# Deformable attention and bottleneck over eight images: x of the next image on GpSimd's queue, q's preparation in four steps, sample transposes half a round later

## The chip, the cores and the metric

The kernel runs on one core of a Trainium2 chip. A core has a matrix engine (TensorE, called PE in the profile, with its weight loads listed as PEld), a vector engine (DVE), an activation engine (ACT), GpSimd (POOL) and SyncE (SP), which here only starts transfers. Each engine works through its own list of instructions in the order in which the program put them there, and an instruction at the head of a list that waits holds up everything behind it. Transfers between HBM and SBUF are started by SP or by POOL and are moved by 16 DMA engines that all of them share.

The metric is the device time of one execution in microseconds (us), the median over several runs. Lower is better.

## The reference, cut to what matters

Two layers work on x, of shape (8, 512, 64, 64): eight images, 512 channels, 4096 pixels. Layer 0 is an attention with sampled keys. Layer 1 is a small bottleneck of convolutions and two dense products.

```python
# layer 0
x0 = groupnorm(x)                                  # 32 groups
q  = w_q @ x0                                      # 512 x 512, per pixel
off = tanh(w_off2 @ gelu(w_off1 * q[:, ::4, ::4])) * 4.0    # 16 x 16 sample places per head
kv = w_kv @ grid_sample_bilinear(q, places(off))   # 256 keys and values
x  = x + w_out @ softmax((q * scale) @ k.T) @ v + b_out     # 8 heads of 64
# layer 1
y = depthwise_conv(conv1x1(groupnorm(x)))          # 512 -> 32 channels, 64x64 -> 32x32
y = fc2(fc1(y))                                    # over the 1024 places
x = x + conv1x1(depthwise_deconv(y))               # 32 -> 512 channels
```

Everything is in float32. The group norm of an image needs the statistics of the whole image before its first q can be computed.

## The kernel before, in words

**Tiling.** An image is held in SBUF as [128 partitions, 4 channel blocks, 4096 pixels] and cut into 8 tiles (`t`) of 512 pixels. There are two such regions and one spare tile for each; image b lives in region b % 2. A tile of x, of q and of the output sits one place further down or up in the same region (`x_tile`, `q_tile`, `out_tile`), so that the stages overwrite each other's input.

**The main loop.** For each image there are 32 rounds (`r`), one per pixel tile and pair of heads (`hp`). A round g emits, in this order: the scaling of earlier results (`scale_two`, every second round before, every other after), the product of weights and values (PE `pa`, L474), the sum of exponentials (PE `pn`, L501, every second round), the logits of the next round (PE `ps`, L456) with their exponentials on ACT (`es`, L464), then, six rounds late (`LAG`), the output projection (PE `pp`, L543) whose result DVE adds to the residual (L550, L553). The residual x is read again from HBM by SP (`load_residual`, L532), and each finished tile is stored by SP (`store`, L556). For tile t of the output these come at r % 4 = 1 (store, first half of the next residual) and r % 4 = 2 (second half).

**Work beside the rounds.** A generator `next_image(b)` gives out other work in small steps. It is called twice in a round: before the output projection (`phase[0] = 0`) and after it (`phase[0] = 1`). I call each call a slot; slot 0 is r = 5, second half, slot 1 is r = 6, first half, and so on. For b = 1 to 6 three things run there:

- `first`: layer 1 of image b-1. Slots 0 to 10 hold its statistics, the product `py` (slot 3, L626), the load of fc1's weights by SP (slot 3, L660, 1 MB), the convolution and the dense products (`pz`, `ph` L690, `pht`, `pu`). In the second halves from slot 12 to slot 26 `project_beside` makes eight output pieces, k = 0 to 7: PE `po` (L766), ACT adds the bias (L791 into one shared half tile called `both`, shown as `spare`, and L796 into two `part` tiles), and POOL starts three transfers of together 1 MB that add the pieces to the output in HBM (L801). `both` is a single buffer, so the L791 of piece k+1 waits until the `both` transfer of piece k has landed. The last piece, k = 7, uses `part` tiles only.
- the loads of x of image n = b+1 (`load_x`, L191), eight of 1 MB, into the region which image b-1 leaves. Before, SP starts them, at slots 5, 8, 9, 10, 11, 12, 16 and 17. Two slots after the last one SP loads w_q (`load_wq`, L135, 1 MB).
- the statistics of x of image n (`norm_x`, L196, 32 operations of DVE, six per second half from slot 12 on, so that they are used up at slot 22), and then three steps of `project_q`: (1) DVE aggregates (`mv`, L167); (2) PE sums over groups (`gps`, L171) and DVE takes differences (`dv`); (3) PE sums again (`gpsb`, L180), DVE adds eps (`ve`, L182), POOL takes the power -0.5 (`gs`, L183), and DVE normalises the first tile of x (L208, four operations). Tiles 1 to 7 are normalised by POOL later.

When `first` is at its end (slot 26), slot 27 emits the whole projection of q as one block (PE `pq`, L251, and the transposes `pqt`, L226), some 125 us on PE, between rounds 19 and 20. In the rounds after it `sample` runs: POOL gathers q by rows (L395), DVE weighs them (`weigh`, L361 to L366), and `to_channels` transposes the result on PE (`pf`, L371), once for each half of the keys. `project_k` (L409) reads them at r = 30.

**What sets the order.** It is written by hand: the program is traced in the order of the calls and each engine gets its own list in that order. A DMA that SP or POOL starts is one entry in that engine's list and waits there for the data, for the buffer, and for the transfer that used the same one of eight counters before, that is the one eight transfers back on the same queue.

Of the kernel before, what the change touches and what calls it, by code (L numbers as in the profile page):

```python
# [19 lines left out]
NCC = C // P  # L20
HW = 64
N = HW * HW
TP = 512
NT = N // TP
# [25 lines left out]
def kernel(  # L50
# [15 lines left out]
    nc = tc.nc  # L66
    xs = x.rearrange("b (cc p) n -> b p cc n", p=P)
# [25 lines left out]
    place = {b: b for b in range(B)}  # L93
    region = {b: b % 2 for b in range(B)}

    def spot(b, k):
        j = region[b]
        k %= NT + 1
        return spares[j] if k == 0 else regions[j][:, :, (k - 1) * TP : k * TP]

    def x_tile(b, t):
        return spot(b, t + 1)
# [59 lines left out]
    def group_stats(st, which, b):  # L162

        nm = f"{which}_{b}"
        mv = small.tile([P, NCC, 2], F32, tag="mv", name=f"mv{nm}")
        for cc in range(NCC):
            nc.vector.bn_aggr(mv[:, cc, :], st[:, cc].rearrange("p t s -> p (t s)"))  # L167
        mean, var = mv[:, :, 0], mv[:, :, 1]
        yield None
        gps = ps_mm.tile([P, TP], F32, tag="mm", name=f"gps{nm}")  # L170
        nc.tensor.matmul(gps[:, :NCC], cst[:, K_GRP : K_GRP + P], mean, start=True, stop=True)  # L171
        gs = small.tile([P, 2, NCC], F32, tag=f"gs{which}", name=f"gs{nm}")
        nc.vector.tensor_copy(gs[:, 0], gps[:, :NCC])
        dv = small.tile([P, NCC], F32, tag="dv", name=f"dv{nm}")
        nc.vector.tensor_sub(dv, mean, gs[:, 0])
        nc.vector.tensor_mul(dv, dv, dv)
        nc.vector.tensor_add(dv, dv, var)
        yield None
        gps2 = ps_mm.tile([P, TP], F32, tag="mm", name=f"gpsb{nm}")
        nc.tensor.matmul(gps2[:, :NCC], cst[:, K_GRP : K_GRP + P], dv, start=True, stop=True)  # L180
        ve = small.tile([P, NCC], F32, tag="ve", name=f"ve{nm}")
        nc.vector.tensor_scalar_add(ve, gps2[:, :NCC], EPS)  # L182
        nc.gpsimd.tensor_tensor(gs[:, 1], ve, nhalf, ALU.pow)  # L183
        return gs
# [1 line left out]

    both_pools = ((t2, "t2"), (gp, "g"))

    def load_x(b, order=range(NT)):
        for t in order:  # L190
            nc.sync.dma_start(x_tile(b, t), xs[place[b]][:, :, t * TP : (t + 1) * TP])  # L191

    def norm_x(b, st, order=range(NT)):
        for t in order:
# [4 lines left out]
    def project_q(b, st, mq, qd, pools):  # L199

        gs = yield from group_stats(st, 0, b)

        qd_px = qd.rearrange("(g h p j) d -> h p g (j d)", g=HEADS, p=P, j=2)

        def normalise(t):
            xt = x_tile(b, t)
            for cc in range(NCC):
                (nc.gpsimd if t else nc.vector).tensor_scalar(  # L208
                    xt[:, cc, :],
                    xt[:, cc, :],  # L210
                    gs[:, 0, cc : cc + 1],
                    gs[:, 1, cc : cc + 1],
                    ALU.subtract,
                    ALU.mult,
                )

        def by_pixel(t, k, bank=(ps_a, "pa")):

            h, ch = divmod(k, 2)
            px = q_tile(b, t)[:, :, 2 * P * h : 2 * P * (h + 1)].rearrange(  # L220
                "p c (n j) -> p c j n", j=2
            )
            pt = bank[0].tile([P, 2, 2 * P], F32, tag=bank[1], name=f"pqt_{b}_{t}_{k}")
            for j in range(2):
                for i in range(2):
                    nc.tensor.transpose(  # L226
                        pt[:, j, i * P : (i + 1) * P], px[:, 2 * ch + i, j, :], ident
                    )
            pool, tag = pools[k % len(pools)]
            qr = pool.tile([P, C], F32, tag=tag, name=f"qr_{b}_{t}_{k}")  # L230
            qr_out = qr.rearrange("p (g j d) -> p j g d", j=2, d=DH)
            qr_in = pt.rearrange("p j (g d) -> p j g d", d=DH)
            if k % 2:
                nc.vector.tensor_copy(qr_out, qr_in)  # L234
            else:
                nc.scalar.copy(qr_out, qr_in)
            nc.sync.dma_start(
                qd_px[2 * t + h, :, 4 * ch : 4 * ch + 4, :],
                qr.rearrange("p (g m) -> p g m", g=4),
            )  # L240

        normalise(0)
        yield None
        for t in range(NT):
            xt, qt = x_tile(b, t), q_tile(b, t)
            if t + 1 < NT:
                normalise(t + 1)
            for oc in range(NCC):
                pq = ps_mm.tile([P, TP], F32, tag="mm", name=f"pq_{b}_{t}_{oc}")
                for cc in range(NCC):  # L250
                    nc.tensor.matmul(  # L251
                        pq,
                        wbuf[:, cc, oc * P : (oc + 1) * P],
                        xt[:, cc, :],
                        start=(cc == 0),
                        stop=(cc == NCC - 1),
                    )
                nc.scalar.copy(qt[:, oc, :], pq)  # L258
                yield 4
                if t:  # L260
                    by_pixel(t - 1, oc)
                    yield 0.64
            if mq is not None:
                nc.vector.tensor_reduce(
                    mq[:, t, :], qt, axis=AX.X, op=ALU.max, apply_absolute_value=True
                )
        for q in range(NQ):
            by_pixel(NT - 1, q, ((ps_a, "pa"), (ps_mm, "mm"))[q % 2])
            yield 0.64
# [8 lines left out]
    def sample(b, qd):  # L278
# [101 lines left out]

        steps = [(h, half, ky) for h in range(2) for half in range(2) for ky in range(2)]

        for slot in range(2 * len(steps) + 3):
            n, odd = divmod(slot, 2)
            if not odd and n >= 5 and n % 4 == 1:
                to_channels(n // 4 - 1)
            if odd and n >= 1:
                weigh(*steps[n - 1], held.pop(0))
            if n < len(steps):
                h, half, ky = steps[n]  # L390
                if not odd:
                    held.append(gp.tile([P, 4, 2, DH], F32, tag="g", name=f"g_{b}_{n}"))
                for i in (2 * odd, 2 * odd + 1):
                    k = h * HEADS + 4 * half + i
                    nc.gpsimd.indirect_dma_start(  # L395
                        held[-1][:, i, :, :].rearrange("p j d -> p (j d)"),
                        None,
                        qd[:, :],
                        bass.IndirectOffsetOnAxis(ap=row[:, ky, k : k + 1], axis=0),
                    )  # L400
            yield None
# [451 lines left out]
    def next_image(b):  # L853

        n = b + 1
        if b:
            free = spot(b - 1, 0)
            first = layer1(b - 1, st1s.pop(b - 1), project_beside, free, free[:, 0:2, :])
            other = iter(())
            if n < B:  # L860
                st = new_stats(0, n)
                blocks = norm_x(n, st)
                other = ready_q(n, st)

            loads = {slot: t for t, slot in enumerate((5, 8, 9, 10, 11, 12, 16, 17))}
            first_block = 12
            ahead = 3
            slot = 0  # L870
            while first:
                if next(first, "end") == "end":
                    first = None
                if n < B:
                    if slot in loads:
                        load_x(n, (loads[slot],))
                    if slot == max(loads) + 2:
                        load_wq()
                    if slot >= first_block and phase[0]:
                        for _ in range(6):  # L880
                            if blocks and next(blocks, "end") == "end":
                                blocks = None
                    if blocks is None and ahead:
                        next(other)
                        ahead -= 1
                slot += 1
                yield None
            yield from other
        if n < B:
            yield from sample(n, qds[n])  # L890
# [10 lines left out]
    with tc.manual_schedule():  # L901
# [13 lines left out]
        for n, step in enumerate(ready_q(0, st)):  # L915
            if n == 3 * NCC:
                st = new_stats(0, 1)
                blocks, other = norm_x(1, st), ready_q(1, st)
            if n >= 3 * NCC and next(blocks, "end") == "end" and 13 * NCC <= n < 13 * NCC + 3:
                next(other)  # L920
        room = 0
        for step in sample(0, qds[0]):
# [7 lines left out]
        for g in range(len(names) + LAG):  # L930
            b, r = divmod(g, ROUNDS)
# [67 lines left out]
    with tc.If(large > 0):  # L999
        with tc.For_i(0, B, 1) as i:  # L1000
            b = "m"
# [94 lines left out]
```

## Time and profile before

| | us |
|---|---|
| median of 3 runs | 3451.34 |
| range of the runs | 3450.25 to 3452.16 |
| the profiled execution, device time | 3462.55 |
| its span, first to last instruction | 3460.8 |
| one image in steady state (`py` at 1891.1 to `py` at 2313.3) | 422.2 |
| idle time of PE before its first `gps`, at the start | 30.0 |

How to read the profile: "busy" is time in which an engine worked. A line of the timeline gives the start in us, the time that the merged instructions took, engine, line and operation, out<-in, the count, and in brackets how long the engine had been idle before it and what ended that wait. A line of the windows view gives a stretch, its length, the busy time of PE, PEld, DVE, ACT and POOL in it, the TensorE clock that was granted (1.00 is full speed), the mean busy share of the 16 DMA engines, and GB/s moved. The list of waits gives who waited for whom, the total, the number of times and the longest.

The page's rows on DMA queues and issues are shown below: packets, MB, and the time their packets took as a share of 16 engines' span (q1 is SP's hardware queue, q0 POOL's software queue); then the loads of x, of which 48 of the 64 belong to the six images in question, and the transfers that add to the output.

```profile
q1 hardware_dynamic: 265712, 312.05, 27.6%
q0 software_dynamic: 39664, 75.53, 12.3%
...
image<-in_x_dram SPq DMA_DIRECT2D x64, 1024.0 KB
...
out_dram<-part POOLq DMA_DIRECT2D x126, 256.0 KB
out_dram<-spare POOLq DMA_DIRECT2D x49, 512.0 KB
```

### The profile page before, as it was taken

How to read it: one execution, taken by the hardware profiler on the slowest of the kernel's cores; microseconds unless marked ns; L12 is line 12 of the kernel's file. 1: busy time of each engine (PE TensorE's matmuls, PEld its weight loads, DVE VectorE, ACT ScalarE, POOL GpSimd, SP SyncE). 2: the span in 40 equal slices, each digit the busy share in tenths (PEclk: the TensorE clock that was granted, in tenths of full speed). 3: DMA queues.
4: the chain of work that ended last, by engine and by line, in shares of the span. 5: the costliest groups of instructions: out<-in, count | busy, mean ns of one | idle time of the engine just before them, and what ended most of it. 6: DMA issues, size and time to landing. Idle time of an engine off the chain costs nothing.

```text
span 3460.8 us, 42052 instructions
## 1 busy us (share of the span) xinstructions
PE 3333.0 (96%) x16660; PEld 1240.7 (36%) x16660; DVE 1895.2 (55%) x2958; ACT 1093.3 (32%) x1512; POOL 931.3 (27%) x685
## 2 busy tenths in 40 slices
PE   6999999999999999999999999999999999999996
PEld 3554223335332352324433244332443324433222
DVE  4433665742757327574275833658246682466565
ACT  1224333332433323333232423324233342332420
POOL 6180400152401614017030170302712027120201
PEclk9999999999999999999999999999999999999996
DMA  7222221662327523275232842329332292322613
GB/s 274 73 79 68 74 74 62 188 154 69 102 82 204 127 76 99 85 216 104 82 98 86 220 96 76 110 74 235 88 96 82 89 250 64 96 76 86 123 38 135
DMA packets 305582, 390.35 MB, mean 113 GB/s; under 512 B 17760, under 2 KB 157280, under 8 KB 305376
## 3 DMA queue, kind: packets, MB, share of 16 engines
q1 hardware_dynamic: 265712, 312.05, 27.6%
q0 software_dynamic: 39664, 75.53, 12.3%
q8 instruction: 132, 2.16, 0.3%
q14 instruction: 74, 0.61, 0.1%
HBM read 193.52 MB, written 192.94 MB: 112 GB/s over the span
## 4 chain that ended last, share of the span: by engine, by line
PE 80%; issue 10%; POOL 3%; DVE 3%; DMA 2%; ACT 1%; SPq 0%; POOLq 0%; DVEq 0%; ACTq 0%
PE pq L251 25%; PE pp L543 20%; PE ps L456 11%; PE pa L474 11%; PE pqt L226 3%; POOL out_dram L801 3%; PE pn L501 3%; PE py L626 2%; PE pk L409 2%; PE pv L436 2%; DMA image<-in_x_dram 1%; PE po L766 1%; DVE rb L527 1%; DVE image L529 0%; PE po L303 0%
## 5 line engine op out<-in xcount | busy, mean ns | idle before, releaser
L251 PE MATMUL pq<-image,wbuf 128*128 128x512 f32 x2048 | 919.9, 594 | 2.4 <-DVE image L208 1.9
L543 PE MATMUL pp<-image,wout 128*64 128x512 f32 x3584 | 827.4, 602 | 19.8 <-DVE image L529 19.0
L464 ACT ACTIVATE es<-ps 128x1024 f32<-128x1024 f32 x512 | 503.5, 1022 | 294.6 <-PE ps L456 212.6
L251 PEld LDWEIGHTS pq<-image,wbuf 128*128 128x128 f32 x2048 | 374.5, 192 | 391.3 <-issue 384.1
L474 PE MATMUL pa<-es,vt 128*64 128x512 f32 x2048 | 490.1, 599 | 4.8 <-ACT es L464 4.8
L395 POOL DMA_INDIRECT g<-qd,row x256 | 272.2, 1063 | 776.7 <-PE pp L543 531.5
L208 POOL TENSOR_SCALAR image<-image,gs 128x512 f32<-128x512 f32 x224 | 465.0, 2653 | 0.4
L456 PE MATMUL ps<-image,kt 64*64 64x512 f32 x3584 | 443.6, 609 | 22.1 <-ACT spare L791 21.7
L543 PEld LDWEIGHTS pp<-image,wout 128*64 128x64 f32 x3584 | 237.2, 137 | 579.7 <-issue 481.0
L234 DVE COPY qr<-pqt 128x512 f32<-128x512 f32 x128 | 88.4, 691 | 634.5 <-PE pqt L226 622.9
L550 DVE SCALAR_TENSOR_TENSOR image<-pp,vec,image 128x512 f32<-128x512 f32 x224 | 167.2, 746 | 441.9 <-PE pp L543 420.4
L486 DVE TENSOR_TENSOR es<-es,es 128x1024 f32<-128x1024 f32 x256 | 310.5, 1213 | 78.8 <-PE pa L474 77.3
L258 ACT COPY image<-pq 128x512 f32<-128x512 f32 x224 | 131.1, 585 | 685.0 <-PE pq L251 665.5
L481 ACT COPY image<-pa 128x512 f32<-128x512 f32 x224 | 131.4, 587 | 617.7 <-PE pa L474 562.7
L183 POOL TENSOR_TENSOR gs<-ve,nhalf 128x4 f32<-128x4 f32 x16 | 22.6, 1414 | 1015.1 <-DVE ve L182 1015.1
L474 PEld LDWEIGHTS pa<-es,vt 128*64 128x64 f32 x2048 | 136.0, 136 | 290.9 <-issue 263.3
L456 PEld LDWEIGHTS ps<-image,kt 64*64 64x64 f32 x3584 | 114.8, 132 | 334.9 <-issue 180.2
L801 POOL DMA_DIRECT2D out_dram<-spare x49 | 59.6, 1217 | 629.8 <-ACT spare L791 623.2
L514 DVE RECIPROCAL rn<-pn 128x512 f32<-128x512 f32 x64 | 214.7, 3354 | 11.8 <-PE pn L501 9.1
L527 DVE STREAM_SHUFFLE rb<-rn 128x512 f32<-128x512 f32 x256 | 186.6, 729 | 0.1
L226 PEld LDWEIGHTS pqt<-ident,image 128*128 128x128 f32 x896 | 137.9, 203 | 100.1 <-issue 89.0
L196 DVE BATCH_NORM_STATS2 st<-image 128x6 f32<-128x512 f32 x256 | 156.8, 677 | 7.7 <-DMA image<-in_x_dram 7.6
(148 smaller groups left out, 2454.7 us busy)
## 6 DMA issues: line engine op xcount, KB each, us to landing
image<-in_x_dram SPq DMA_DIRECT2D x64, 1024.0 KB
qd<-qr SPq DMA_DIRECT2D x256, 256.0 KB
image<-in_x_dram SPq DMA_DIRECT2D x112, 512.0 KB
out_dram<-image SPq DMA_DIRECT2D x49, 1024.0 KB
out_dram<-part POOLq DMA_DIRECT2D x126, 256.0 KB
out_dram<-spare POOLq DMA_DIRECT2D x49, 512.0 KB
wbuf<-in_w_kvT_dram SPq DMA_DIRECT2D x14, 1024.0 KB
spare<-in_x_dram SPq DMA_DIRECT2D x16, 512.0 KB
```

The lines of the kernel that those rows point to most:

```text
L208: (nc.gpsimd if t else nc.vector).tensor_scalar(xt[:, cc, :], xt[:, cc, :], gs[:, 0, cc : cc + 1], gs[:, 1, cc : cc + 1], ALU.subtract, AL ...
L226: nc.tensor.transpose(pt[:, j, i * P : (i + 1) * P], px[:, 2 * ch + i, j, :], ident)
L251: nc.tensor.matmul(pq, wbuf[:, cc, oc * P : (oc + 1) * P], xt[:, cc, :], start=(cc == 0), stop=(cc == NCC - 1),)
L395: nc.gpsimd.indirect_dma_start(held[-1][:, i, :, :].rearrange("p j d -> p (j d)"), None, qd[:, :], bass.IndirectOffsetOnAxis(ap=row[:, ky, ...
L456: nc.tensor.matmul(ps[k : k + DH, a, :], kt[r : r + DH, hp, kc * P + k : kc * P + k + DH], qt[r : r + DH, hp, :], start=True, stop=True,)
L464: nc.scalar.activation(e, ps, AF.Exp)
L474: nc.tensor.matmul(pa[a * DH : (a + 1) * DH, :], vt[:, kc, hd * DH : (hd + 1) * DH], es[kc][:, a, :], start=(kc == 0), stop=(kc == 1),)
L486: nc.vector.tensor_add(es[0], es[0], es[1])
L514: nc.vector.reciprocal(rn, denominators.pop((b, t)))
L527: nc.vector.stream_shuffle(rb, rn, [2 * (hp % 2) + hp // 2] * 32)
L543: nc.tensor.matmul(pp[r : r + DH, :], wout[:, hp, oc * P + r : oc * P + r + DH], ao[:, hp, :], start=(hp == 0), stop=(hp == NCC - 1),)
L550: nc.vector.scalar_tensor_tensor(xt[:, oc, :], pp, col(V_BOUT + oc), xt[:, oc, :], ALU.add, ALU.add)
```

## The change

The diff has three parts.

1. `load_x` takes a queue. In `next_image` the eight loads of x are started by POOL, one in each of the slots 5 to 12, where SP had started them at 5, 8 to 12, 16 and 17. `load_wq` stays at slot 19 (5 + 8 + 6) and on SP.
2. `project_q` gets one more `yield` ahead of the first normalisation, so that its preparation has four steps: the normalisation of the first tile is a step of its own. The steps stand at the head of a slot, ahead of `first`, where they had stood at its end. The statistics still end in slot 22, so the steps come in slots 23, 24, 25 and 26 where they had come at the end of 22, 23 and 24. The prologue takes four steps instead of three as well.
3. In `sample` the transposes `to_channels` move from the even slot 2n to the odd slot 2n+1 (n = 5 and 9), and there is one more slot in the loop. The condition of `weigh` is written anew so that nothing is weighed in the additional slot.

```diff
-    def load_x(b, order=range(NT)):
+    def load_x(b, order=range(NT), queue=nc.sync):
         for t in order:
-            nc.sync.dma_start(x_tile(b, t), xs[place[b]][:, :, t * TP : (t + 1) * TP])
+            queue.dma_start(x_tile(b, t), xs[place[b]][:, :, t * TP : (t + 1) * TP])
@@ project_q
+        yield None
         normalise(0)
         yield None
@@ sample
-        for slot in range(2 * len(steps) + 3):
+        for slot in range(2 * len(steps) + 4):
             n, odd = divmod(slot, 2)
-            if not odd and n >= 5 and n % 4 == 1:
+            if odd and n >= 5 and n % 4 == 1:
                 to_channels(n // 4 - 1)
-            if odd and n >= 1:
+            if odd and 1 <= n <= len(steps):
                 weigh(*steps[n - 1], held.pop(0))
@@ next_image
-            other = iter(())
+            other, blocks = iter(()), ()
...
-            loads = {slot: t for t, slot in enumerate((5, 8, 9, 10, 11, 12, 16, 17))}
+            first_load = 5
             first_block = 12
-            ahead = 3
+            ahead = 4
             slot = 0
             while first:
+                if blocks is None and ahead:
+                    next(other)
+                    ahead -= 1
                 if next(first, "end") == "end":
                     first = None
                 if n < B:
-                    if slot in loads:
-                        load_x(n, (loads[slot],))
-                    if slot == max(loads) + 2:
+                    if first_load <= slot < first_load + NT:
+                        load_x(n, (slot - first_load,), nc.gpsimd)
+                    if slot == first_load + NT + 6:
                         load_wq()
                     if slot >= first_block and phase[0]:
                         for _ in range(6):
                             if blocks and next(blocks, "end") == "end":
                                 blocks = None
-                    if blocks is None and ahead:
-                        next(other)
-                        ahead -= 1
                 slot += 1
                 yield None
@@ prologue
-            if n >= 3 * NCC and next(blocks, "end") == "end" and 13 * NCC <= n < 13 * NCC + 3:
+            if n >= 3 * NCC and next(blocks, "end") == "end" and 13 * NCC <= n < 13 * NCC + 4:
                 next(other)
```

In the lists of the engines this gives, for each of six images: POOL's list has seven loads of x between its `gs` of layer 1 and the three transfers of piece k = 0, and the eighth after these three; SP's list has no load of x; DVE's aggregation, differences and first normalisation stand later, the first normalisation behind the L550 and L553 of round 18 and no longer ahead of two `scale_two` pairs; PE's `gps` stands just ahead of the `po` of piece 6, and `gpsb` ahead of the output projection of round 18; `pf` stands after the logits of the next round and ahead of its output projection.

## Prediction

> **What bounds the kernel now.** I read the busy table first, then the list of waits, then the timelines of PE, ACT, DVE, POOL and SP through one image, and last the windows, for what the DMA engines do meanwhile. PE is busy 3333.0 of 3460.8 us. Of its 127.8 us without work 30.0 lie at the start; the rest is what an edit of order can win, with the half clock that follows a gap. The list of waits:
>
> ```profile
> PE 3333.0 (96%) x16660; PEld 1240.7 (36%) x16660; DVE 1895.2 (55%) x2958; ACT 1093.3 (32%) x1512; POOL 931.3 (27%) x685
> ...
> ACT spare L791 <- DMA out_dram<-spare: 74.6, 11, 8.2
> ...
> DVE image L208 <- POOL gs L183: 33.1, 8, 5.4
> ...
> PE ps L456 <- ACT spare L791: 21.7, 8, 3.8
> ...
> PE pp L543 <- DVE image L529: 19.0, 15, 2.3
> ```
>
> PE waits for `both` (21.7 us) and for DVE L529 (19.0), and DVE stood before L529 for `gs` of POOL (33.1). In the third image:
>
> ```profile
> 1965.08 1.94 PE L474 MATMUL pa<-es,vt 128*64 128x512 f32 x8
> ...
> 1969.52 2.74 PE L456 MATMUL ps<-image,kt 64*64 64x512 f32 x16 [2.50 <-ACT spare L791]
> 1972.19 4.80 PE L543 MATMUL pp<-image,wout 128*64 128x512 f32 x16
> 1976.93 1.14 PE L766 MATMUL po<-spare,outw 32*128 32x512 f32 x8
> ...
> 2001.16 1.94 PE L543 MATMUL pp<-image,wout 128*64 128x512 f32 x8
> 2005.10 3.56 PE L543 MATMUL pp<-image,wout 128*64 128x512 f32 x8 [2.00 <-DVE image L529]
> 2008.58 1.16 PE L766 MATMUL po<-spare,outw 32*128 32x512 f32 x8
> ```
>
> A stall costs its gap and a slow stretch after it (`pp` 4.80 for some 3.65, `ps` 2.74 for 1.95). So I measure each by how much longer its round is than one without a stall, over the six images:
> - Stall 1 (piece k = 3): `pa` to `po` 1965.08 to 1976.93 is 11.85 us, where an unstalled round has 7.33. Excess 4.67, 3.09, 5.48, 4.51, 3.12, 5.32: 26.2 us.
> - Stall 2 (k = 4), in the second and fifth image only: 3.69 + 3.83 = 7.5 us.
> - Stall 3 (first normalisation): `pp` 2001.16 to 2008.58 is 7.42, against 3.58. Excess 3.20, 2.86, 2.86, 3.84, 2.85, 2.88: 18.5 us.
> - Stall 4: `pf` waits for `weigh`, 7.8 us, with no slow clock after it.
>
> ```profile
> L371 PE MATMUL pf<-ident,image 128*128 128x128 f32 x64 | 11.7, 290 | 7.8 <-DVE image L366 7.8
> ```
>
> Behind stall 3 is DVE's wait for POOL's L183 (2.21 us, from 1999.51); behind stall 1 a transfer:
>
> ```profile
> 2001.76 1.92 DVE L208 TENSOR_SCALAR image<-image,gs 128x512 f32<-128x512 f32 x4 [5.06 <-POOL gs L183]
> ```
> ```profile
> 1968.36 1.11 ACT L791 ACTIVATE spare<-po,vec 128x1024 f32<-128x1024 f32 x1 [6.96 <-DMA out_dram<-spare]
> ```
>
> SP had put 5 MB beside that 1 MB of k = 2 (a store 1, residual halves 0.5 each, x 2, w_q 1):
>
> ```profile
> 1955.82 0.38 SPq L556 DMA_DIRECT2D out_dram<-spare  x1
> 1956.30 0.45 SPq L532 DMA_DIRECT2D image<-in_x_dram  x1
> 1956.80 2.38 SPq L191 DMA_DIRECT2D image<-in_x_dram  x2
> 1959.28 0.76 SPq L532 DMA_DIRECT2D image<-in_x_dram  x1
> 1960.14 0.72 SPq L135 DMA_DIRECT2D wbuf<-in_w_qT_dram  x1
> ```
>
> The windows (PE, PEld, DVE, ACT, POOL, clock, DMA share, GB/s) show loads of x alone, then pieces alone, then both:
>
> ```profile
> 1930.00:1935.00 5.00, 5.00 (x32) 1.43 (x30) 4.79 (x12) 1.61 (x2) 0.00 (x0) 1.00 1.05 388
> 1950.00:1955.00 5.00, 5.00 (x32) 1.37 (x24) 4.89 (x9) 2.05 (x2) 1.56 (x2) 1.00 1.04 154
> 1965.00:1970.00 5.00, 2.50 (x16) 0.69 (x16) 5.00 (x8) 1.65 (x3) 0.24 (x1) 1.00 1.10 265
> ```
>
> **What the Trainium skill says.** "DMA: Bandwidth & Descriptors", Queues, rings and completion order: each DMA engine goes round the queue rows that have work, packet by packet. The trace agrees: mixed, 265 GB/s lie between 388 and 154. The same page, Issuing engines are not separate DMA queues: another issuing engine gives no other DMA engines. "SBUF — State Buffer", SBUF: two separate sides: some DVE operations keep GpSimd from writing descriptors, and a transfer that it starts then appears blocked. The trace of before cannot confirm it for loads, as POOL starts none there. "TensorE: Matmul & The Clock Gate", What's actually happening: half clock after an idle window of about 3.4 us. Here it follows gaps of 2.0 and 2.5 us already; the measurement decides.
>
> **The change part by part.**
>
> *Preparation of q.* No operation is added; `gps` comes a step later, L208 three slots later. After it, POOL's 2.21 us begin with `gpsb` ahead of `pp` of round 18, which takes 3.65 us, and L208 stands behind the L550 and L553 of that round, which wait for this `pp` anyway. So the 5.06 us of DVE's wait lie under `pp`. L208 takes 1.92 us and, with an L550 (0.75) ahead of it, ends some 3.5 us after `pp`; PE comes to the projection of q 4.8 us after `pp`, behind an L474 and L456. That is 1.3 us to spare; if it fails, the price is its excess, under 2 us an image. Stall 3 goes: 18.5 us. What is late next is the second exponential on ACT, 5.06 us after, for which DVE's L486 is ready at 4.7.
>
> *`pf` half a round later.* Behind `ps` (1.95 us) the result of `weigh` has been there (the longest wait was 1.75 for a pair). The copies behind `pf` end some 2.6 us after it, `pk` reads them at 4.3. Stall 4 goes: 7.8 us.
>
> *The loads.* SP's list loses 48 issues, POOL's gains them. POOL has room: it waited 49.23 us before piece k = 0.
>
> ```profile
> 1939.03 1.38 POOL L801 DMA_DIRECT2D out_dram<-spare  x1 [49.23 <-ACT spare L791]
> ```
>
> An L801 of half a load's size takes 1.2 to 1.4 us, so seven loads are 7 x 1.2 = 8.4 us if the issue doesn't grow with size, 7 x 2.4 = 17 if it does: hidden. Behind a load that waits stand only loads and k = 0. Nothing holds POOL to the slots of the code, since slots order lists and not times: x0 to x6 need only PE past `py` and the old stores landed, which I read as 1894.5 to 1898, not 1900 to 1927. 7 MB at 2.7 us each (388 GB/s) are 19 us: they end about 1917. Their bound on the other side is the skill's price for a transfer that GpSimd starts ("DMA: Bandwidth & Descriptors", Bandwidth): 6.15 us for 1 MB, thus 43 us, to 1938, an estimate. I take 19 us, as the 16 engines are the same. x7 stands behind k = 0 and runs from about 1942 to 1948, when k = 1 starts (1948.6).
>
> In the stretch 1895 to 1917 the engines had room before (in 1898 to 1906 the windows give a DMA share of 0.41), but fc1's weights run there, for this product:
>
> ```profile
> 1914.66 1.07 PE L690 MATMUL ph<-spare,wbuf 128*32 128x256 f32 x16
> ```
>
> The weights are issued at 1898.15 and a load of them lands in 6.91 us elsewhere in the chain of waits. With half of the engines they need some 10 to 14 us at most and are there by 1912, before 1914.66. The small transfers for `rn` (1912.9 to 1914.8) come at the end of the burst; DVE has about 2.2 us free after them. Cost between 0 and 8.2 us an image (below); I take 0.
>
> *Does stall 1 go?* Ahead of k = 2's landing SP keeps 3 MB without x (store, residuals, w_q). Up to that landing at 1968.36, of 12.5 us at 260 GB/s (3.2 MB), 1 MB with its slower adds took about a third of the packets, and SP's queue had moved only some 2.7 MB. So as long as SP has 2.7 MB or more queued, the piece has the same share and lands at the same time. Another piece, k = 6, issued at 1997.67 beside 2 MB of SP (a store and two residual halves), landed at about 2009.3, 11.6 us later, as k = 2's 11.4.
>
> w_q stays at slot 19, where it meets k = 2 as before. Bounds for stall 1: nothing wins 0, all 26.2; I take 0. Stall 2 needs a backlog of more than 3 MB and goes: 7.5 us (bounds 0 and 7.5).
>
> *Sum.* 18.5 + 7.8 + 7.5 = 33.8 us. The profiled device time is 3462.55 (span 3460.8, and 1.75 around it), 11.2 above the median; 3462.55 - 33.8 = 3428.8, and against the median 3451.3 - 33.8 = 3417.5 us.
>
> **Rivals.**
> - *Stall 1 goes too.* For it: SP's queue is 2 MB shorter when k = 2 lands. Against: k = 6 above. All four stalls: 60.0 us, 3391.3.
> - *The early burst costs a part.* x7 delays k = 1 (an L791 has 1.6 us to spare there), or `rn` comes late to DVE. Of 33.8, 10 to 25 us stay: 3426 to 3441.
> - *Slower: fc1's weights are starved.* One mechanism: the burst of 7 MB holds the engines, and 1 MB on SP's queue lands only when it is through, about 1921. PE's list stands at `ph` for 1921 - 1914.7 = 6.3 us, with 1.9 for the half clock 8.2 us, six times 49: 3451.3 - 33.8 + 49 = 3467. It decides from 33.8 / 6 = 5.6 us an image. For it: nothing spreads the loads out, and the price of 43 us would last beyond `ph`. Against: engines go round the queues.
> - *The change does nothing for PE:* the gaps move to the next wait, 3451. Against: three of the four have slack of 1 us or more behind them.
>
> **How the numbers follow.** A measurement here tells 0.2%, 6.9 us, from no change. Forecast 0.58, its own range 3407 to 3425 (stall 1 shortened by up to 10 us below; above, stall 2 left); stall 1 gone 0.12; burst costs a part 0.15; weights starved 0.11; nothing 0.04. The range takes in the two faster rivals and leaves out 0.15 with the last two: 3390 to 3441. Faster 0.58 + 0.12 + 0.15 = 0.85, same 0.04, slower 0.11.
>
> **What would show it.** After: DVE L208 no longer waits for `gs`, and PE `pp` not for L529; the row of `pf` has no idle time; POOL issues x0 to x6 at about 1895 in the third image and `ph` does not wait for its weights; ACT L791 still waits 6 to 7 us at k = 3, and PE `ps` for it about 15 us in all. I am wrong if `ph` or DVE L527 waits more, if x7 pushes k = 1 back, or if the wait of `ps` for L791 is gone.

## The result, and the profile after

The changed kernel is slower: 3463.2 us (median of 8 runs, 3459.65 to 3464.47) against 3451.0 (8 runs of before), a ratio of 1.0034 with a 95% interval of 1.0023 to 1.0045. That is 12 us more, where 34 less were forecast. Of the later experiments' executions two slow ones, of 4939.5 and 5605.6 us at granted clocks of 0.65 and 0.57, are not counted. Line numbers of the changed kernel are one higher from L251 on: L791 is now L792, L796 is L797, L527 is L528.

The page's busy table and the list of waits (who waited for whom, total, number, longest) of the changed kernel:

```profile
PE 3344.5 (97%) x16660; PEld 1246.7 (36%) x16660; DVE 1897.0 (55%) x2958; ACT 1092.1 (32%) x1512; POOL 966.7 (28%) x733
```
```profile
ACT es L465 <- DVE es L487: 82.9, 33, 5.4
...
ACT spare L792 <- DMA out_dram<-spare: 43.4, 6, 8.1
...
DVE rb L528 <- DMA rn<-rn: 31.9, 9, 4.4
...
PE ps L457 <- ACT spare L792: 16.6, 6, 3.6
...
PE po L767 <- ACT es L465: 12.5, 6, 2.1
ACT part L797 <- DMA out_dram<-part: 10.8, 12, 2.1
PE ps L457 <- ACT part L797: 10.1, 6, 2.5
```

Three waits that were to go are gone from the six images: L208 no longer waits for `gs`, `pp` no longer for L530, and `pf` no longer for `weigh`. In their place PE waits in each of the six images twice anew: `po` for an exponential (12.5 us) and `ps` for the `part` copies (10.1). The same list of the kernel before has DVE's wait for `rn` at 11.9 us, and neither `po` for L464 nor `ps` for L796 among PE's waits:

```profile
ACT es L464 <- DVE es L486: 65.0, 35, 2.9
...
DVE rb L527 <- DMA rn<-rn: 11.9, 9, 2.7
```

To see where the time went, I cut each of the six image periods at PE's `po` of each piece and summed each stage over the six images of one profiled execution, in us. "k0" is the stretch from `po` of k = 0 to `po` of k = 1. The last stage is cut once more, at the end of the projection's `pq` and `pqt`.

| stage | before | after | difference |
|---|---|---|---|
| `py` to k0 | 272.2 | 272.2 | 0 |
| k0 | 57.2 | 82.1 | +24.9 |
| k1, k2, k5 | 160.6 | 160.6 | 0 |
| k3 (stall 1) | 76.6 | 78.8 | +2.2 |
| k4 (stall 2) | 63.9 | 56.4 | -7.5 |
| k6 (stall 3) | 76.7 | 58.3 | -18.4 |
| k7 to the projection of q | 28.9 | 41.0 | +12.1 |
| the projection of q | 760.6 | 764.9 | +4.3 |
| its end to the next `py` (`pf`) | 1042.7 | 1031.6 | -11.1 |
| six periods | 2539.4 | 2545.9 | +6.5 |

So all that was to be removed was removed: 18.4, 7.5 and 11.1 us, where 18.5, 7.5 and 7.8 were forecast. Two new losses outweigh it: 24.9 us at k0, and 12.1 + 4.3 = 16.4 us at k7 and in the projection behind it.

**The first loss: `rn` behind the burst.** POOL starts x0 to x6 at once, as forecast (timeline of POOL, third image, changed kernel):

```profile
1890.57 0.84 POOL L191 DMA_DIRECT2D image<-in_x_dram  x1 [5.20 <-PE py L627]
1894.03 4.54 POOL L191 DMA_DIRECT2D image<-in_x_dram  x6 [2.62 <-PE py L627]
1936.42 1.27 POOL L802 DMA_DIRECT2D out_dram<-spare  x1 [37.86 <-ACT spare L792]
```

The windows (length, busy time of PE, PEld, DVE, ACT, POOL, clock, DMA share, GB/s) show the 16 engines full until about 1914:

```profile
1902.00:1906.00 4.00, 4.00 (x24) 1.06 (x16) 3.89 (x6) 1.74 (x2) 0.00 (x0) 1.00 1.02 384
1906.00:1910.00 4.00, 4.00 (x28) 1.20 (x26) 3.96 (x5) 1.03 (x2) 0.00 (x0) 1.00 1.03 388
1910.00:1914.00 4.00, 4.00 (x34) 1.48 (x32) 1.20 (x2) 1.86 (x3) 0.00 (x0) 1.00 1.04 390
1914.00:1918.00 4.00, 4.00 (x26) 1.16 (x20) 2.41 (x6) 0.58 (x1) 0.00 (x0) 1.00 0.19 71
```

SP issues the four small transfers for `rn` (4 KB each) at 1908.47, inside the burst. From there to DVE's L528, which reads them, it took 3.7 us before (1912.91 to 1916.60) and takes 7.0 us now. The records of single packets show where: in all six images the first packet of a transfer comes about 4.1 us after its issue, where it came 1.2 us after it before. The difference of 2.9 us is close to the 2.7 us in which one load of 1 MB passes at 388 GB/s. That a transfer waits for about one load is my reading of these two numbers; no run tests it with loads of another size. DVE's list is then 3 us late for 17 us on end, and passes that to ACT and PE (timelines of DVE, ACT and PE, changed kernel):

```profile
1915.47 0.01 DVE L528 LOAD_MASK_SELECT rb<-rn  x1 [4.27 <-DMA rn<-rn]
...
1932.78 1.22 DVE L487 TENSOR_TENSOR es<-es,es 128x1024 f32<-128x1024 f32 x1
```
```profile
1934.10 1.02 ACT L465 ACTIVATE es<-ps 128x1024 f32<-128x1024 f32 x1 [5.38 <-DVE es L487]
1935.02 1.11 ACT L792 ACTIVATE spare<-po,vec 128x1024 f32<-128x1024 f32 x1
```
```profile
1931.99 1.13 PE L767 MATMUL po<-spare,outw 32*128 32x512 f32 x4
1935.17 1.85 PE L767 MATMUL po<-spare,outw 32*128 32x512 f32 x4 [2.05 <-ACT es L465]
1936.95 3.68 PE L475 MATMUL pa<-es,vt 128*64 128x512 f32 x8
```

Read from the bottom: the second half of `po` needs the bank of PSUM that the second exponential reads; that exponential overwrites the tile which L487 adds; L487 stands in DVE's list behind everything that waited for `rn`. From `py`, L487 came at 43.1 us before and at 46.2 now. So PE is late by the same 3.0 us: the second half of `po` begins 3.18 us after the first in the third image, where it began 0.15 us after it before. (The gap shows as 2.05 us only, because the halves otherwise overlap.) In three images that is all. In the three others the clock falls to half behind the gap, for 3.4, 3.4 and 6.8 us, and the loss is 4.7, 4.7 and 6.3 us; in the third image, shown here, `pa` takes 3.68 us for 1.94.

**The second loss: k = 7 behind k = 6.** With stall 3 gone PE comes to k = 7 earlier, and ACT's L797 meets the `part` tiles of k = 6, which POOL had started to send from 2000.24 on (timeline of ACT, then of PE, changed kernel):

```profile
2007.83 1.26 ACT L797 ACTIVATE part<-po,vec 128x512 f32<-128x512 f32 x2 [3.91 <-issue]
2011.14 0.69 ACT L797 ACTIVATE part<-po,vec 128x512 f32<-128x512 f32 x1 [2.05 <-DMA out_dram<-part]
2012.41 0.69 ACT L797 ACTIVATE part<-po,vec 128x512 f32<-128x512 f32 x1 [0.57 <-DMA out_dram<-part]
```
```profile
2009.54 1.09 PE L457 MATMUL ps<-image,kt 64*64 64x512 f32 x8
2013.15 1.25 PE L457 MATMUL ps<-image,kt 64*64 64x512 f32 x8 [2.52 <-ACT part L797]
```

Before, L796 of k = 7 came 12.2 us after k = 6's first issue (1997.67 to 2009.84) and waited for nothing. Now it comes 8.3 us after it (1999.53 to 2007.83). The packets say why k = 6 takes so long: SP has just issued a store and two residual halves, 2 MB, and from 2000 to 2005 SP's queue alone moves data (from 1998 to 2003 before). Then come the 0.5 MB of `both`, and the `part` tiles behind it. In three images the clock falls to half where the projection begins, which is the 4.3 us of the table.

### The profile page after: what moved, and what is told of

The parts are those of the page before. It is cut to its first block, busy times and chain, and to the rows that moved or that the text cites. A ratio compares the mean times of both kernels' runs of the same rounds, so it can differ in the third digit from the quotient of the medians.

```text
span 3461.6 us, 42078 instructions
## 1 busy us (share of the span) xinstructions
PE 3344.5 (97%) x16660; PEld 1246.7 (36%) x16660; DVE 1897.0 (55%) x2958; ACT 1092.1 (32%) x1512; POOL 966.7 (28%) x733
## 4 chain that ended last, share of the span: by engine, by line
PE 78%; issue 11%; DVE 4%; DMA 4%; POOL 2%; ACT 1%; SPq 0%; POOLq 0%; ACTq 0%; DVEq 0%
PE pq L252 25%; PE pp L544 20%; PE ps L457 10%; PE pa L475 10%; PE pqt L226 3%; PE pn L502 3%; POOL out_dram L802 2%; DMA out_dram<-part 2%; PE py L627 2%; PE pk L410 2%; PE pv L437 2%; DMA spare<-in_fc_wT_dram 1%; PE po L767 1%; DMA rn<-rn 0%; DVE wbuf L674 0%
## 5 line engine op out<-in xcount | busy, mean ns | idle before, releaser
L208 POOL TENSOR_SCALAR image<-image,gs 128x512 f32<-128x512 f32 x224 | 461.8, 2140 | 0.5
L487 DVE TENSOR_TENSOR es<-es,es 128x1024 f32<-128x1024 f32 x256 | 310.7, 1214 | 71.6 <-PE pa L475 71.5
L528 DVE STREAM_SHUFFLE rb<-rn 128x512 f32<-128x512 f32 x256 | 187.4, 732 | 0.1
```

Of the source, the lines that this page charges most:

```text
L208: (nc.gpsimd if t else nc.vector).tensor_scalar(xt[:, cc, :], xt[:, cc, :], gs[:, 0, cc : cc + 1], gs[:, 1, cc : cc + 1], ALU.subtract, AL ...
L487: nc.vector.tensor_add(es[0], es[0], es[1])
L528: nc.vector.stream_shuffle(rb, rn, [2 * (hp % 2) + hp // 2] * 32)
```

## The experiments

All ratios are to the kernel before on the same chip; the kernel before took between 3451 and 3473 us on the chips used, and 3459 and 3471 in two sessions on one of them, so ratios are compared. 0.1% is 3.5 us.

**The loads back on SP** (changed kernel; the other two parts kept):

```diff
-            first_load = 5
+            loads = {slot: t for t, slot in enumerate((5, 8, 9, 10, 11, 12, 16, 17))}
...
-                    if first_load <= slot < first_load + NT:
-                        load_x(n, (slot - first_load,), nc.gpsimd)
-                    if slot == first_load + NT + 6:
+                    if slot in loads:
+                        load_x(n, (loads[slot],))
+                    if slot == max(loads) + 2:
```

> The changed kernel with the loads of x back on SP at the old slots 5, 8 to 12, 16, 17; preparation in four steps and pf half a round later are kept. Theory T (the seven loads in a row on POOL delay the small transfers for rn, DVE is 3 us late, PE po of piece k=0 waits for the second exponential: about 25 us over six images; the preparation only swaps its stall for a wait of piece k=7 for the part tiles of k=6): DVE L528 waits about 1 us for rn as before, no gap in po of k=0, the wait of PE for ACT L797 at k=7 stays, the time is 10 to 20 us under before, 3431 to 3441. Rival R (the preparation is what costs, the loads are harmless): the time stays at 3460 or above.

Measured: 0.9954 (0.9939 to 0.9970), 16 us under before. DVE's wait for `rn` is back at 11.8 us in all, k0 at 57.3 us. The wait at k = 7 stays (`ps` for L797 10.1 us, k7 40.4). T holds, R falls.

**Only the loads moved** (kernel before): the first part of the change, without the other two.

```diff
+                    if first_load <= slot < first_load + NT:
+                        load_x(n, (slot - first_load,), nc.gpsimd)
```

> The kernel before with only the loads of x moved to POOL. T: the gap in po of k=0 is there (2.05 us an image and in some images a half clock), stall 2 of k=4 is gone: 25 - 7.5 = +17, so 3463 to 3473. R: 3444 to 3451.

Measured: 1.0050 (1.0035 to 1.0066), +17 us. Its list of waits:

```profile
ACT es L464 <- DVE es L486: 81.6, 33, 5.4
...
DVE rb L527 <- DMA rn<-rn: 31.8, 9, 4.4
```

The wait for `rn` is that of the changed kernel; k0 is 83.5 us, k4 56.4 (stall 2 gone), k7 29.9. T holds.

**Only the preparation** (kernel before):

```diff
+        yield None
         normalise(0)
...
-            ahead = 3
+            ahead = 4
...
+                if blocks is None and ahead:
+                    next(other)
+                    ahead -= 1
                 if next(first, "end") == "end":
```

> The kernel before with only the fourth step of the preparation, first in its slot. T: DVE L208 waits no more for POOL, PE pp not for DVE L530; but piece k=7 comes 2 us earlier and its ACT L797 waits for the part transfers of k=6, which land 11.6 us after their issue as before. Net 0 to -6 us: 3445 to 3451. R: +10 us or more, 3461 and above. If the full 18.5 us come out (3432), the wait of k=7 needs the loads on POOL.

Measured: 0.9986 (0.9976 to 0.9995), 5 us less. The stages show the exchange: k6 58.3 for 76.7, k7 42.7 for 28.9, the projection 2.2 us more, and PE's wait at k = 7 is there without any load on POOL:

```profile
ACT part L797 <- DMA out_dram<-part: 12.0, 12, 1.9
PE ps L457 <- ACT part L797: 11.4, 6, 2.6
```

**Only `pf`** (kernel before):

```diff
-            if not odd and n >= 5 and n % 4 == 1:
+            if odd and n >= 5 and n % 4 == 1:
```

> The kernel before with only the transposes pf half a round later. T: 7.8 to 11 us less, 3440 to 3443, and nothing else moves. R': the time of the profiled execution of before (3462) was not typical and its stalls of pf are not in the timed runs: 3449 to 3451.

Measured: 0.9970 (0.9958 to 0.9981), 10 us less. T holds. (In the profiles with the old order of `pf` taken later, PE's wait there is 10.1 to 10.5 us; the 7.8 of the first was the lowest.) This and the preparation alone make 15.3 us; together (the loads back on SP) they made 15.9. The loads alone and the rest alone sum to +1.4 us where the change has +12, with 5 us of uncertainty on each of the two and 4 on the third, which was measured on another chip. Why they differ stays open.

**Half of the burst** (changed kernel): four loads on POOL, four on SP behind `rn`.

```diff
-                        load_x(n, (slot - first_load,), nc.gpsimd)
+                        load_x(n, (slot - first_load,), nc.gpsimd if slot < 9 else nc.sync)
```

> The changed kernel with x0 to x3 on POOL in slots 5 to 8, and x4 to x7 on SP in slots 9 to 12. T: 4 MB and fc1's weights are through at about 1907 (13.5 us at 388 GB/s), before the rn transfers are issued at 1908.5; DVE L528 waits about 1 us for them, the stage k=0 to k=1 returns from 82 to 57 us over six images: 25 us under the changed kernel, ratio to before 0.996 (the loads on SP all lie ahead of k=2, so stall 2 stays gone). Rival S (what delays rn is that POOL starts loads at all, by DVE keeping GpSimd from its descriptors or the like, not the bytes in flight): DVE's wait for rn stays at 4 us, ratio 1.003.

Measured: 0.9950 (0.9937 to 0.9962). POOL still starts four loads at the same point of the image, and the engines are free again ahead of `rn`, which SP issues at 1901.25 in this profile (windows, then DVE's timeline):

```profile
1894.00:1898.00 4.00, 4.00 (x30) 1.20 (x24) 3.82 (x8) 1.94 (x2) 0.00 (x0) 1.00 1.03 388
1898.00:1902.00 4.00, 4.00 (x24) 1.14 (x24) 3.96 (x3) 0.58 (x1) 0.00 (x0) 1.00 0.36 135
1902.00:1906.00 4.00, 4.00 (x38) 1.34 (x32) 3.03 (x6) 2.32 (x3) 0.00 (x0) 1.00 0.03 8
```
```profile
1904.90 0.01 DVE L528 LOAD_MASK_SELECT rb<-rn  x1 [0.92 <-DMA rn<-rn]
```

The wait is 0.92 us, the first packet comes 1.2 us after its issue again, and k0 is 57.2. It is the bytes in flight when `rn` is issued, not that POOL starts loads: S falls. k7 stays at 41.8, since nothing here touches it.

**w_q later** (changed kernel):

```diff
-                    if slot == first_load + NT + 6:
+                    if slot == 22:
```

> The changed kernel with the load of w_q at slot 22 in place of 19, beside piece k=4. T (stall 1 is set by the bytes that SP's queue moves beside k=2: 3 MB now, 2 MB then): both of k=2 lands 9.8 us after its issue, as that of k=6 does, in place of 11.4: the gap of PE falls from 2.5 us to under 1 and often no half clock follows: 8 to 18 us under the changed kernel, ratio 0.998 to 1.001. Rival U (the share between the queues, not the bytes that stand behind, sets it): both of k=2 lands as before, ratio 1.0034 as the changed kernel.

Measured: 1.0039 (1.0026 to 1.0052), as the changed kernel. The time missed T's, though its mechanism is there: L792 of k = 3 comes 10.2 us after k = 2's issue, where it was 11.3, and k3 falls from 78.8 to 64.7 us. But w_q now stands in SP's list behind the `rn` transfers, goes out at 1987.47 in the third image, just as piece k = 5 does, and the late pieces wait (ACT's timeline, k = 6 and 7 of the third image):

```profile
1996.44 1.12 ACT L792 ACTIVATE spare<-po,vec 128x1024 f32<-128x1024 f32 x1 [5.58 <-DMA out_dram<-spare]
...
2009.16 0.69 ACT L797 ACTIVATE part<-po,vec 128x512 f32<-128x512 f32 x1 [2.98 <-DMA out_dram<-part]
```

k6 rises by 2.3 and k7 by 8.4 us: k = 6 is sent later, so k = 7 waits longer. Here the pieces hang together like a chain: the megabyte taken from one was paid at another.

**Parts first** (changed kernel), for piece k = 6 alone:

```diff
+            if k + 2 == 2 * NCC:
+                parts = parts[1:] + parts[:1]
             for block, part in parts:
                 nc.gpsimd.dma_start(block, part, accum_op=ALU.add)
```

> The changed kernel, in which POOL starts for piece k=6 its two part transfers ahead of both (piece k=7 uses no both). T (k=7 waits for the part transfers of k=6, which stand behind 0.5 MB of both on POOL's queue): they land 3 to 4 us earlier, ACT L797 waits no more, the stage k=7 to pq returns from 41 to 29 us, and with the half clock of pq 12 to 16 us come off: ratio 0.999 to 1.000. Rival V (k=7 waits for something else, or the part transfers land no earlier beside 2 MB of SP): 1.0034 as the changed kernel.

Measured: 0.9982 (0.9973 to 0.9991), 18 us under the changed kernel by the two ratios, give or take 5, and 12 to 16 were expected. L797 of k = 7 runs through (timeline of ACT, third image):

```profile
2006.13 2.42 ACT L797 ACTIVATE part<-po,vec 128x512 f32<-128x512 f32 x4 [3.91 <-issue]
```

k7 is 29.5 for 41.0, and the projection is back at 760.6. SP's 2 MB are still there, so what decided was the order on POOL's queue, where 0.5 MB of `both`, which k = 7 doesn't use, stood ahead. V falls.

**All three edits:** half of the burst, w_q at slot 22, parts first.

> The three edits together: half of the loads on SP, w_q at slot 22, part transfers of k=6 first. T: the sum, 25 + 13 + 14 = 52 us under the changed kernel, 40 under before: ratio 0.988 (0.986 to 0.991). If the later edits only move the wait to another piece (k=4 beside w_q, say), 0.992 or more.

Measured: 0.9885 (0.9871 to 0.9899): 40 us under before, 3419.8 against 3459.0. k0 57.3, k3 60.6, k6 61.2, k7 31.5, and no stretch of half clock in the six images.

**All three, with w_q early:**

```diff
-                    if slot == 22:
+                    if slot == 14:
```

> The three edits together, but with the load of w_q at slot 14, beside piece k=1, where SP has nothing else queued, in place of slot 22. T: neither k=2 nor k=6 has w_q beside it; the stages k=6 and k=7 to pq lose the 3 us and 2.5 us that they have in the kernel with all three edits, k=3 stays: ratio to before 0.987 (all three edits: 0.9885). If x4 to x7 and w_q together now reach into the time of k=1 or k=2, the stage k=2 or k=3 grows by 5 us or more and the ratio is 0.990 or above.

Measured: 0.9874 (0.9857 to 0.9891), 3425.3 against 3470.6. k6 and k7 are at 58.3 and 28.9, the lowest seen, as T had it. But w_q goes out just behind other `rn` transfers and only 7 us before SP's store, and k2 and k3 take 3 us more each. The two versions can't be told apart; both beat before by 1.0% or more, by the ends of their intervals.

**The kernel before once more,** for a second profile:

> The kernel before once more, for a second profile: if the profiled execution of before was slow for reasons of its own (more stretches at half clock), this one has another number of them and a span within some us of the median of its runs; the stages k=0 to pq keep their sums within 5 us.

Measured: 3467.8 us where the runs of before on this chip have 3470.6; k0 57.2, k3 77.6, k4 59.1, k6 77.7, k7 31.8. The largest of these differences is 4.8 us (k4). So the stages are those of the kernel and not of one execution; only stall 2 is worth less here, 2.7 us for 7.5. That the first profile of before was 11 us above its median stays unexplained; on which of the chips it was taken isn't known.

## Why the prediction was wrong

- *Step that failed first: "The small transfers for `rn` ... come at the end of the burst; DVE has about 2.2 us free after them. Cost between 0 and 8.2 us an image (below); I take 0."* By the prediction's own times, issue from 1912.9 and a burst to 1917, they lay 4 us inside the burst; in the run it was 6 us. They took 3.3 us longer. And the 2.2 us of slack, for which the prediction names no consumer, weren't there. The first consumer is the second half of `po`, through its bank of PSUM, and the timeline of PE in the profile of before gave a sign that it had none:

```profile
1936.43 1.27 PE L766 MATMUL po<-spare,outw 32*128 32x512 f32 x8
```

  This `po` of k = 0 took 1.27 us where those of other pieces take 1.14 to 1.16: its second half already came 0.13 us late, too little for the list. In the changed kernel L487 is 3.0 us late and so is this half, so any delay of DVE there is PE's. It measured 24.9 us in the profiles, where 0 was taken. The rival "the burst costs a part" named `rn`, at a cost of 9 to 24 us (it leaves 10 to 25 of the 33.8), with a chance of 0.15; and a longer wait of L527 stood among the signs of being wrong.

- *Step that failed second: "Stall 3 goes: 18.5 us. What is late next is the second exponential on ACT".* The stall went (18.4), but what was late next was k = 7's `part` tiles, 12.1 us, with 4.3 in the projection. The number needed was in the prediction: it had k = 6 landing 11.6 us after its issue, and used that only to argue on stall 1. Stall 3 itself had been the time in which k = 6 could land. Preparation alone gives 5 us of the 18.5 (shown by the third experiment), and the seventh shows that the order on POOL's queue decides it.

- *Stall 1 stays:* right, 78.8 for 76.6. That it hangs on what SP still has queued beside k = 2 agrees with w_q's move (64.7). But the working, a third of the packets from the issue on, isn't what the trace shows: in the kernel before, from 1958 to 1963, SP's queue takes 101% of the engines' time and POOL's none, and only then do the two go packet for packet (272 and 271 packets from 1964 to 1968). In the changed kernel SP's queue is alone from 1960 to 1965. The mean rate of 265 GB/s, which the prediction took as a sign of turns, doesn't show this. And the 11.6 us of k = 6 weren't those of `both`, which landed 10.1 us after its issue; its `part` tiles came after it. So the answer was right partly by luck. *Stall 2 goes:* right; -7.5 against the profile from which the forecast was read, -2.7 against the second profile of before.

- *`pf`:* right in kind. Alone it gave 10 us (6.6 to 14.5), where the wait was 7.8 in the profile used.

- *Bandwidth and issue:* right: 7 MB of x with 1 MB of weights took from about 1892 to 1915, at 384 to 392 GB/s once the queues were full. The other end of the bound, 43 us from the Trainium skill ("DMA: Bandwidth & Descriptors", Bandwidth: 6.15 us for a transfer of 1 MB), doesn't hold here: x0, at first alone on the engines, moved in 3.7 us (1892.1 to 1895.8), and those in the row passed in 2.7 each; the measurement decides. In the same page's Issuing engines are not separate DMA queues the trace agrees: from POOL's queue they filled the same 16 engines and SP's small transfers felt it.

- *Slower rival:* fc1's weights were not starved; `ph` came 23.6 us after `py` in both kernels. They had an easy case: SP issued them at 1893.71, just ahead of x1 to x6 (from 1894.03), and from 1896 to 1898 SP's queue alone moved data. That the measured 3463 is near this rival's 3467 is chance, since its mechanism didn't occur.

- *The sum over the whole:* six periods differ by 6.5 us in the two profiles, while the runs differ by 12. The first `py` came at 615.7 us in the profile of the changed kernel and at 620.8 to 623.7 in the profiles of all the others, with and without the four-step preparation, so that execution had a better start. Of these profiles it is the only one known to be from the chip on which the kernel before takes 3451 us; whether that is the reason isn't shown.

## What to carry to other kernels

- A stretch in which the DMA engines are idle isn't free for a burst if a small transfer on the critical chain falls into it: place the bulk behind it, or so that it ends before it. Here four loads fitted and seven did not, and the price was a delay of some 3 us an image, without the half clock.
- Take slack from the first consumer, buffers included, and look for instructions a tenth of a microsecond longer than their like: here one such had none.
- A stall is also the time in which something else lands. Before a stall is removed, set the landing times of every transfer behind it against the new times of who reuses its buffer.

## What the runs showed of the hardware

- POOL's issue of a load of 1 MB took 0.75 to 0.84 us, less than an L801 of half the size (1.2), so that the estimate of 8.4 to 17 us for seven was too high: 5.4.
- Four transfers of 4 KB on SP's queue beside a full burst on POOL's took 7.0 us from first issue to use, where 3.7 is usual. Each one's first packet was 2.9 us later than usual, and they were served before the burst was over.
- A transfer that came just behind 2 MB or more on the other queue moved nothing at first, and had no share of the engines: POOL's 1 MB of k = 2 from 1958 to 1963 (before) and of k = 6 from 2000 to 2005 (changed kernel).
- A gap's price isn't fixed. The same gap of some 2.05 us at k = 0 cost 3.0 to 3.1 us in the three images in which no half clock followed, 4.7 where it lasted 3.4 us and 6.3 where it lasted 6.8, in one execution. Over the six images half clock took 23.8 us before and 47.6 us in the changed kernel. With all three edits gaps of up to 2.1 us, and with w_q early of up to 2.4, were followed by none.
